# The SSM's input by channel in runs of 32 numbers, a gathered stationary operand, and state matrices in 2 KB rows

## Chip, cores and metric

The kernel runs on one core of one Trainium2 chip. The metric is device time in microseconds. The kernel before took 1888.09 us (median of three runs, 1886.04 to 1891.85).

## What is computed

`x` has 8 sequences of 2048 positions and 256 channels, in float32. Three sublayers follow each other:

```python
x = x + 0.5 * ffn(layernorm(x), w1, b1, w2, b2)      # 256 -> 1024 -> 256, relu
x = x + attn(layernorm(x))
x = x + 0.5 * ffn(layernorm(x), w1, b1, w2, b2)      # the same weights

def attn(u):        # a state space model (S4D): a long convolution by channel
    K[h, l] = 2 Re(sum_n Ct[h, n] exp(dt[h] A[h, n] l))      # 64 complex states n per channel
    y = causal convolution of u with K along the positions
    r = u + y + u * D
    return layernorm(r) * ln_w + ln_b
```

## The kernel before

**Two feed-forwards and the SSM between them.** The 2048 positions are cut into 16 chunks of 128; a chunk of one sequence is a column, so there are 128 columns, and 64 groups of two columns. `sublayer` (L807) runs a feed-forward over the groups. A group has 8 steps, each one block of 128 of the hidden layer: six matmuls (L788) into a PSUM bank, relu and a rounded copy `hh` on ACT (L857, L858), the remainder `hl` on DVE (L859); three steps later six matmuls (L798) take `hh` and `hl` to the output. `hh` and `hl` have four slots each. In the first feed-forward (letter a) `post_a` then adds the residual (L905), normalises each column (L696 on DVE, L692 on ACT in the first 12 groups) and writes it to `u`. In the second (letter b) `pre_b` reads columns of `u` from the last to the first: their statistics (L663) and a scaling (the instructions shown at L118).

**`u`** (L127) holds the SSM's input, later its output in place, as [position in chunk, chunk, sequence, channel], 128 KB per partition. A channel's 128 numbers on a partition lie 1024 bytes apart. Until the columns are written, quarters of `u` serve as room for making the SSM's matrices: `room[2]` and `room[3]` are the third and fourth quarters of the chunks.

**The matrices** are made during the first feed-forward by the generator `matrices` (L234). For each of 32 batches of 8 channels, POOL multiplies tables (`make`, L570 to L580), the result is stored (`o_dram`) and transposed by DMA through 16-bit planes (`spread`, `turn`, L590 to L605), put together again by a copy on DVE and one on ACT (`transpose`, L620, kept in program order) and stored as `pt_dram`. The generator yields how much of the feed-forward its work is to be spread over; `sublayer` adds 1.32 to a clock per step and takes work from the generator up to it. At certain groups (`due`) all the work up to a mark is issued at once if it has not come yet: the mark "half" (the matrices of the first half, which lie in `room[2]`) at group 39, "tables" at group 48. The clock decides the order of the program. The framework's scheduler may then reorder instructions that are not kept in order.

**The SSM** works on pairs of channels, in 12 groups of 8 or 16 pairs (`PLAN`, L920), whose states lie in three buffers A, B and E.
- `states(gr)` (L964): for each batch of 4 pairs and each channel c of the pair, `pt` is loaded (256 KB) and four float32 matmuls (L970) stream `u`'s channel through it: 15 chunks of 8 sequences, 120 columns. ACT keeps the result (L957).
- `scan` (L987): 14 steps over the chunks, of four small instructions (L1005 to L1008), some pairs on DVE and some on POOL. On DVE its two temporaries come from slots `hh` and `hl`, or, every other group, from `e` and `te`.
- `outputs(gr)` (L1019): for each batch and c, four matmuls (L1036) with `u`'s channel as the stationary operand and the near lags `tz` as the moving one, and four (L1041) with the states and `ot`; ACT writes the bank back to `u` (L1045). `ot` and `tz` are loaded before, 256 KB each.

The program has the states of groups 1, 2 and 3 first, and then outputs of a group and states of the group three later in turns. The states of group 0 come early, at the end of the first feed-forward (`early`, L1050, matmuls L1072). Each float32 matmul shows as two in the profile (64 batches x 4 x 2 = 512 for L1036). Loads and stores are issued by SP in one queue.

Of the kernel before, what the change touches and what calls it, by code (L numbers as in the profile page):

```python
# [10 lines left out]
F32 = mybir.dt.float32  # L11
F32R = mybir.dt.float32r
# [17 lines left out]
# pi / 2 in four parts, the first three of eight bits each  # L30
# [13 lines left out]
def macaron_s4d_kernel(  # L44
# [63 lines left out]
    BUFS = {"e": 1, "te": 1, "x": 5, "xn": 1, "xh": 2, "xl": 2, "hh": 4, "hl": 4, "pl": 2, "g": 1, "gt": 1}  # L108
# [11 lines left out]
    def ts(o, a, s0, op0, s1, op1):  # L120
# [5 lines left out]
    # The SSM's input, then its output in place: [position in chunk, chunk, batch, channel].  # L126
    u = upool.tile([P, NJ, B, H], F32, name="u")  # L127
    # Until their quarters of the input come: room for the SSM's matrices.
    room = [
        u[:, i * JQ : (i + 1) * JQ].rearrange("p j b h -> p (j b h)") for i in range(NQ)  # L130
    ]

    # ------------------------------------------------------------- weights
# [61 lines left out]
    # w**128, and its imaginary part with the signs for the conjugate states  # L195
# [27 lines left out]
    def vsqrt(o, v, t, s, pace):  # L223
        """o = sqrt(v), to float32's precision."""
# [9 lines left out]
    def matrices():  # L234
        S1 = 0.9              # two steps of 128 columns
        S2 = 1.35             # two steps of 256 columns
# [7 lines left out]
        # ---- parameters: (c, n) to the partitions  # L244
# [23 lines left out]
        # w and w**16: exp(dt A) and exp(16 dt A)  # L268
# [18 lines left out]
        # (no effect but where float32 holds no fraction of the phase)  # L287
# [19 lines left out]
        # the quadrant: q mod 4 as f in -2..2, cos = 1 - |f|, sin = f (2 - |f|)  # L307
# [12 lines left out]
        # w = rho (cs + i sn)(cq + i sq)  # L320
# [25 lines left out]
        # w**128  # L346
# [5 lines left out]
        # Ct = C (w - 1) / A, doubled  # L352
# [30 lines left out]
        # p0 = sqrt(2 Ct w)  # L383
# [28 lines left out]
        yield from vsqrt(fa, v, tt, s, S1)      # the larger part over sqrt(big)  # L412
# [19 lines left out]
        # ---- lag 0, with the skip and the residual: K[0] + 1 + D  # L432
# [23 lines left out]
        # ---- w**(16 a) and p0 w**b  # L456
# [27 lines left out]
        # ---- lags 128 to 1: Re(sum_n p0 w**(16 a) p0 w**b), eight pairs to a product, of  # L484
        # which the blocks on the diagonal count
# [71 lines left out]
        def make(bt):  # L557
            """P of a batch of channels."""
# [24 lines left out]
        def spread(bt):  # L583
            """Stores it, and turns its planes."""
# [28 lines left out]
        def transpose(bt):  # L613
# [3 lines left out]
            pu = ptb.bitcast(U16).rearrange("p (s r n w) -> p w r s n", s=BCH, r=2, w=2)  # L617
            plv = pl.rearrange("p w (r s n) -> p w r s n", r=2, n=N)
# [37 lines left out]
    # ------------------------------------------------------------ the sublayers  # L656
# [13 lines left out]
    def root(mv, name):  # L670
        """half of sqrt(var + eps)"""
# [4 lines left out]
    def rstds(mv, s, name):  # L676
        """1 / sqrt(var + eps), the root improved by a step."""
# [23 lines left out]

    def ucols(g):
        c0 = g * NTB
        return [u[:, (c0 + i) // B, (c0 + i) % B, :] for i in range(NTB)]
# [4 lines left out]
    def ffn_in(xt, name, on_act=False, by_dma=False):  # L709
        """Normalises xt and transposes it, in two parts; xt gets half the second bias."""  # L710
# [31 lines left out]
    def turn_by_dma(xn, name):  # L742
        """The transposes by the DMA engines: of the numbers' upper and lower halves."""
# [63 lines left out]
    def sublayer(w1t, w2t, pre, post, lead, tag, first=(), background=(), due=()):  # L807
        """A feed-forward over all groups. pre(g) makes a group's input in steps, the last
        of them `lead` steps after the first, just before the group's turn; post(g) takes
        its output in steps. `first` is work for the steps before the first group;  # L810
        `background` fills gaps: all of it up to a mark comes before the output of the
        group that `due` has for the mark."""
# [4 lines left out]
        last = {}             # the background is not to come before these  # L817
# [27 lines left out]
        for t in range(-lead, NG * SLOTS + LAG + 1):  # L845
# [3 lines left out]
            if t >= 0 and g < NG:  # L849
                fc = 2 * k + f  # L850
                hh = slot("hh", [P, TOK], f"hh_{tag}{g}_{fc}", F32R)
                hl = slot("hl", [P, TOK], f"hl_{tag}{g}_{fc}", F32R)
                pend[g, fc] = hh, hl
                ph = bank("h", f"ph_{tag}{g}_{fc}")[:, 0:TOK]
                up(w1t, xT[g], ph, fc)
                # the hidden block stays in PSUM until it is split
# [33 lines left out]
    # ---- x1 = x + ffn(norm(x)) / 2; u = norm(x1)  # L890
    ACT_NORM = 12         # groups during which the vector engine has the parameters to make
# [36 lines left out]
    TAGS = ("hh", "hl"), ("e", "te")  # L928
# [9 lines left out]
    # how many steps each group's scan keeps behind the one before it  # L938
# [15 lines left out]
    def keep(xs, pv, c, p0, cols):  # L954
        """The chunks' own states from PSUM: the pair's channels one below the other."""
# [6 lines left out]
    def states(gr):  # L962
        xs = states_of(gr)
        for p0, bt, c in batches(gr):  # L964
            pt = slot("x", [P, PB, P], f"pt{bt}_{c}")
            nc.sync.dma_start(out=pt, in_=pt_dram[bt].rearrange("k (l c m) -> k l c m", c=2, m=P)[:, :, c])
            pv = bank("tbo"[(2 * bt + c) % 3], f"pv{bt}_{c}")
            pv = pv[:, 0 : PB * CB].rearrange("p (l m) -> p l m", l=PB)
            for l in range(PB):
                nc.tensor.matmul(  # L970
                    pv[:, l, :], pt[:, l, :], u[:, 0 : NJ - 1, :, BCH * bt + 2 * l + c],
                    start=True, stop=True,
                )
            keep(xs, pv, c, p0, slice(B, NJ * B))
# [12 lines left out]
    def scan(gr, E, p0, p1, j0, j1, tags):  # L987
        """state of a chunk += conj(w**128) times the state of the chunk before it"""
# [6 lines left out]
        for j in range(j0, j1):  # L995
            t1, t2 = (
                slot(tag, [P, 2, 8 if tag in ("g", "gt") else 16, B], f"{tag}_{gr}_{j}")[:, :, 0:n] for tag in tags
            )
# [14 lines left out]
    def stack(xs, pairs, sw):  # L1013
        """Puts each channel's real and imaginary parts one below the other."""
# [4 lines left out]
    def outputs(gr):  # L1019
        xs = states_of(gr)  # L1020
        for p0, bt, c in batches(gr):
# [6 lines left out]
            # tz[k, l, 127 - i] = K[i - k]  # L1028
# [4 lines left out]
            )  # L1033
            py = bank("h", f"py{bt}_{c}").rearrange("p (l m) -> p l m", l=PB)
            for l in range(PB):
                nc.tensor.matmul(  # L1036
                    py[:, l, :], u[:, :, :, BCH * bt + 2 * l + c].rearrange("p j b -> p (j b)"), tz[:, l, :],
                    start=(l == 0), stop=False, skip_group_check=True,
                )
            for l in range(PB):  # L1040
# [5 lines left out]
                u[:, :, :, BCH * bt + c : BCH * (bt + 1) : 2],  # L1046
                py.rearrange("p l (j b) -> p j b l", b=B),
            )

    def early():  # L1050
# [138 lines left out]
```

## Time and profile before

| | before |
|---|---|
| runs, median (lowest to highest) | 1888.09 us (1886.04 to 1891.85) |
| profiled execution, span | 1885.0 us, granted clock 0.987 |
| PE busy (matmuls) | 1813.4 us, 96% |
| DVE, ACT, POOL busy | 1566.6, 1267.4, 726.0 us |
| DMA moved | 245 MB, 130 GB/s over the span |
| first feed-forward | to about 866 us (last L905) |
| SSM's stage, first L970 to last L1041 | 843 to 1125 us |
| second feed-forward | from about 1131 us |

Of the profiled execution the span is given, from its first to its last instruction; the runs' median lies 3.1 us above it. A row of the profile's groups names the line of the kernel, the engine, the operation, output and inputs by the program's names and their shape. PE is TensorE's matmuls, PEld its weight loads, which overlap the matmuls. SP is the queue that issues the DMAs.

### The profile page before, as it was taken

How to read it: one execution, taken by the hardware profiler on the slowest of the kernel's cores; microseconds unless marked ns; L12 is line 12 of the kernel's file. 1: busy time of each engine (PE TensorE's matmuls, PEld its weight loads, DVE VectorE, ACT ScalarE, POOL GpSimd, SP SyncE). 2: the span in 40 equal slices, each digit the busy share in tenths (PEclk: the TensorE clock that was granted, in tenths of full speed). 3: DMA queues.
4: the chain of work that ended last, by engine and by line, in shares of the span. 5: the costliest groups of instructions: out<-in, count | busy, mean ns of one | idle time of the engine just before them, and what ended most of it. 6: DMA issues, size and time to landing. Idle time of an engine off the chain costs nothing.

```text
span 1885.0 us, 41022 instructions
## 1 busy us (share of the span) xinstructions
PE 1813.4 (96%) x14091; PEld 1797.2 (95%) x14091; DVE 1566.6 (83%) x5027; ACT 1267.4 (67%) x3027; POOL 726.0 (39%) x963
## 2 busy tenths in 40 slices
PE   7999899889989999999999988999999999999999
PEld 7998889889988999999999988999999999999998
DVE  5999897988899867757666648999888999999995
ACT  6776556767767767766566645767777776677775
POOL 1117753888488115111866621222222222222220
PEclk9999999999999999999999998999999999999999
DMA  5111224798879743345667681333333333333331
GB/s 188 45 45 50 80 80 129 215 251 243 242 224 254 207 107 94 92 118 162 174 179 198 183 246 51 91 90 94 94 94 90 92 95 90 92 94 91 93 93 52
DMA packets 329140, 245.31 MB, mean 130 GB/s; under 512 B 170467, under 2 KB 275683, under 8 KB 328419
## 3 DMA queue, kind: packets, MB, share of 16 engines
q1 hardware_dynamic: 327152, 241.76, 45.9%
q8 instruction: 111, 1.82, 0.4%
q0 software_dynamic: 800, 0.67, 0.2%
q14 instruction: 99, 0.80, 0.1%
q10 hardware_dynamic: 978, 0.26, 0.1%
HBM read 91.89 MB, written 111.15 MB: 108 GB/s over the span
## 4 chain that ended last, share of the span: by engine, by line
PE 65%; DVE 2%; DMA 1%; issue 0%; ACT 0%; DVEq 0%; ACTq 0%
PE po_b L798 19%; PE ph_b L788 19%; PE po_a L798 7%; PE ph_a L788 6%; PE py L1036 6%; PE pv L970 5%; PE py L1041 3%; DMA tz<-kpad 1%; PE pe L1072 0%; DVE hl_a L859 0%; DVE xb L118 0%; DVE st_r L663 0%; DVE u L620 0%; DVE y L118 0%; DVE u L696 0%
## 5 line engine op out<-in xcount | busy, mean ns | idle before, releaser
L788 PE MATMUL ph_a<-xh_a,wa 128*128 128x256 f32 x2048 | 460.2, 289 | 7.6 <-ACT xh_a L735 3.7
L788 PE MATMUL ph_b<-xh_b,wb 128*128 128x256 f32 x2048 | 442.4, 284 | 0.7 <-ACT xh_b L735 0.7
L798 PE MATMUL po_a<-wa,hh_a 128*128 128x256 f32 x2048 | 393.3, 285 | 0.0
L798 PE MATMUL po_b<-wb,hh_b 128*128 128x256 f32 x2048 | 387.5, 283 | 0.0
L788 PEld LDWEIGHTS ph_a<-xh_a,wa 128*128 128x128 f32 x2048 | 361.7, 196 | 9.2 <-ACT xh_a L735 5.6
L857 ACT ACTIVATE ph_a<-ph_a,b_sb 128x256 f32<-128x256 f32 x512 | 228.8, 449 | 189.5 <-PE ph_a L788 179.1
L788 PEld LDWEIGHTS ph_b<-xh_b,wb 128*128 128x128 f32 x2048 | 352.5, 193 | 1.1 <-ACT xh_b L735 1.1
L857 ACT ACTIVATE ph_b<-ph_b,b_sb 128x256 f32<-128x256 f32 x512 | 230.3, 451 | 162.2 <-PE ph_b L788 151.4
L798 PEld LDWEIGHTS po_a<-wa,hh_a 128*128 128x128 f32 x2048 | 323.2, 194 | 0.2 <-issue 0.2
L798 PEld LDWEIGHTS po_b<-wb,hh_b 128*128 128x128 f32 x2048 | 319.2, 192 | 0.0
L788 PE MATMUL ph_a<-xl_a,wa 128*128 128x256 f32 x1024 | 294.4, 290 | 20.7 <-DVE xl_a L769 11.2
L798 PE MATMUL po_a<-wa,hl_a 128*128 128x256 f32 x1024 | 299.6, 293 | 9.0 <-DVE hl_a L859 8.5
L1125 POOL TENSOR_TENSOR xb<-xb,lnb_sb 128x512 f32<-128x512 f32 x64 | 94.4, 1475 | 530.6 <-DMA xb<-x_dram 329.0
L798 PE MATMUL po_b<-wb,hl_b 128*128 128x256 f32 x1024 | 292.7, 286 | 0.3 <-DVE hl_b L859 0.2
L788 PE MATMUL ph_b<-xl_b,wb 128*128 128x256 f32 x1024 | 286.5, 284 | 0.1
L859 DVE TENSOR_TENSOR hl_a<-ph_a,hh_a 128x256 fp32r<-128x256 f32 x512 | 206.9, 411 | 82.6 <-ACT hh_a L858 80.9
L859 DVE TENSOR_TENSOR hl_b<-ph_b,hh_b 128x256 fp32r<-128x256 f32 x512 | 205.1, 410 | 37.6 <-ACT hh_b L858 36.0
L788 PEld LDWEIGHTS ph_a<-xl_a,wa 128*128 128x128 f32 x1024 | 201.3, 197 | 23.1 <-DVE xl_a L769 12.2
L719 POOL TENSOR_TENSOR xa<-xa,hb 128x512 f32<-128x512 f32 x64 | 84.3, 1317 | 350.6 <-DVE xn_a L696 239.3
L798 PEld LDWEIGHTS po_a<-wa,hl_a 128*128 128x128 f32 x1024 | 198.5, 194 | 14.4 <-DVE hl_a L859 14.0
L798 PEld LDWEIGHTS po_b<-wb,hl_b 128*128 128x128 f32 x1024 | 196.3, 192 | 1.6 <-DVE hl_b L859 0.8
L788 PEld LDWEIGHTS ph_b<-xl_b,wb 128*128 128x128 f32 x1024 | 197.2, 193 | 0.4 <-DVE xl_b L737 0.3
(281 smaller groups left out, 3589.7 us busy)
## 6 DMA issues: line engine op xcount, KB each, us to landing
xa<-in_L_attn_x_dram SPq DMA_DIRECT2D x64, 256.0 KB, 2.8
x_dram<-xa SPq DMA_DIRECT2D x64, 256.0 KB, 2.3
o<-u SPq DMA_DIRECT2D x64, 256.0 KB, 4.0
pv<-planes SPq DMA_DIRECT2D x32, 512.0 KB, 3.5
pt<-u SPq DMA_DIRECT2D x32, 512.0 KB, 3.6
ot<-o SPq DMA_DIRECT2D x64, 256.0 KB, 3.5
tz<-kpad SPq DMA_DIRECT2D x64, 256.0 KB, 3.8
xb<-x_dram SPq DMA_DIRECT2D x64, 256.0 KB, 2.8
```

The costliest lines, as they stand in the source:

```text
L719: G_.tensor_add(xt, xt, hb2.unsqueeze(1).to_broadcast([P, NTB, H]))
L788: nc.tensor.matmul(ph, wt[wp][:, dc, fs], xp[:, dc, :], start=(n == 0), stop=(n == 3 * NDC - 1))
L798: nc.tensor.matmul(po[:, i, :], hp[:, tsl], wt[wp][:, fc, :], start=(fc == 0 and i == 0 and n == 0), stop=(fc == NFC - 1 and n == 2), skip ...
L857: A_.activation(ph, ph, AF.Relu, bias=b1_sb[:, fc : fc + 1])
L859: last[V] = V.tensor_sub(hl, ph, hh.bitcast(F32))
L970: nc.tensor.matmul(pv[:, l, :], pt[:, l, :], u[:, 0 : NJ - 1, :, BCH * bt + 2 * l + c], start=True, stop=True,)
L1036: nc.tensor.matmul(py[:, l, :], u[:, :, :, BCH * bt + 2 * l + c].rearrange("p j b -> p (j b)"), tz[:, l, :], start=(l == 0), stop=False, s ...
L1041: nc.tensor.matmul(py[:, l, :], xs[:, c, p0 + l, :], ot[:, l, :], start=False, stop=(l == PB - 1), skip_group_check=True,)
L1125: G_.tensor_add(xt, xt, lnb_sb.unsqueeze(1).to_broadcast([P, NTB, H]))
```

## The change

- `u` becomes [position in chunk, quarter, channel, 32 columns]: a channel's 128 numbers on a partition lie in four runs of 32. A column's 256 channels now lie 128 bytes apart, and a column spreads over the whole of its quarter.
- L970's matmuls stream all four runs, 128 columns in place of 120; the last 8 are not kept.
- In `outputs` a DVE copy gathers the four channels of a batch into a contiguous tile `uc` ([128, 4, 128]), which is then the stationary operand of L1036.
- `hh` and `hl` become the two halves of one tile `hx` with four slots. The scan's temporaries on every other group, and `uc`, come from `hx` too.
- `pt_dram` is put in the order (c, pair, column) instead of (pair, c, column): a load of `pt` takes 2 KB in a row from each partition's row instead of four times 512 bytes. The copies of L620 write in that order.
- The mark "half" is due at group 32 instead of 39.

Everything else is as it was. The core of the diff, without removed comments:

```diff
-    BUFS = {"e": 1, "te": 1, "x": 5, "xn": 1, "xh": 2, "xl": 2, "hh": 4, "hl": 4, "pl": 2, "g": 1, "gt": 1}
+    BUFS = {"e": 1, "te": 1, "x": 5, "xn": 1, "xh": 2, "xl": 2, "hx": 4, "pl": 2, "g": 1, "gt": 1}
...
-    u = upool.tile([P, NJ, B, H], F32, name="u")
+    CQ = JQ * B
+    u = upool.tile([P, NQ, H, CQ], F32, name="u")
...
+    room = [u[:, i].rearrange("p h m -> p (h m)") for i in range(NQ)]
...
-            pu = ptb.bitcast(U16).rearrange("p (s r n w) -> p w r s n", s=BCH, r=2, w=2)
-            plv = pl.rearrange("p w (r s n) -> p w r s n", r=2, n=N)
+            pu = ptb.bitcast(U16).rearrange("p (c l r n w) -> p w r l c n", c=2, r=2, n=N, w=2)
+            plv = pl.rearrange("p w (r l c n) -> p w r l c n", r=2, c=2, n=N)
...
+    def column(c):
+        return u[:, c // CQ, :, c % CQ]
...
-                hh = slot("hh", [P, TOK], f"hh_{tag}{g}_{fc}", F32R)
-                hl = slot("hl", [P, TOK], f"hl_{tag}{g}_{fc}", F32R)
-                pend[g, fc] = hh, hl
+                hx = slot("hx", [P, 2, TOK], f"hx_{tag}{g}_{fc}", F32R)
+                hh, hl = pend[g, fc] = hx[:, 0], hx[:, 1]
...
-    TAGS = ("hh", "hl"), ("e", "te")
+    TAGS = ("hx",), ("e", "te")
...
-            nc.sync.dma_start(out=pt, in_=pt_dram[bt].rearrange("k (l c m) -> k l c m", c=2, m=P)[:, :, c])
+            nc.sync.dma_start(out=pt, in_=pt_dram[bt].rearrange("k (c l m) -> k c l m", c=2, m=P)[:, c])
...
-                    pv[:, l, :], pt[:, l, :], u[:, 0 : NJ - 1, :, BCH * bt + 2 * l + c],
+                    pv[:, l, :], pt[:, l, :], u[:, :, BCH * bt + 2 * l + c, :],
...
-            keep(xs, pv, c, p0, slice(B, NJ * B))
+            keep(xs, pv[:, :, 0:CB], c, p0, slice(B, NJ * B))
...
+            if tags == ("hx",):
+                both = slot("hx", [P, 2, 2, 16, B], f"hx_{gr}_{j}")
+                t1, t2 = (both[:, i, :, 0:n] for i in range(2))
...
+            mine = u[:, :, BCH * bt + c : BCH * (bt + 1) : 2, :]
+            uc = slot("hx", [P, PB, P], f"uc{bt}_{c}")
+            V.tensor_copy(
+                uc.rearrange("p l (q m) -> p l q m", q=NQ), mine.rearrange("p q l m -> p l q m")
+            )
...
-                    py[:, l, :], u[:, :, :, BCH * bt + 2 * l + c].rearrange("p j b -> p (j b)"), tz[:, l, :],
+                    py[:, l, :], uc[:, l, :], tz[:, l, :],
...
             A_.copy(
-                u[:, :, :, BCH * bt + c : BCH * (bt + 1) : 2],
-                py.rearrange("p l (j b) -> p j b l", b=B),
+                mine.rearrange("p q l m -> p l q m"),
+                py.rearrange("p l (q m) -> p l q m", q=NQ),
             )
...
-        {"half": 39, "tables": NG * 3 // 4},
+        {"half": NG // 2, "tables": NG * 3 // 4},
```

More of the change, by code (lines that the diff above doesn't have):

```diff
@@ L124, in macaron_s4d_kernel @@
     make_identity(nc, ident)
-    u = upool.tile([P, NJ, B, H], F32, name="u")
-    room = [
-        u[:, i * JQ : (i + 1) * JQ].rearrange("p j b h -> p (j b h)") for i in range(NQ)
-    ]
+    CQ = JQ * B
+    u = upool.tile([P, NQ, H, CQ], F32, name="u")
+    room = [u[:, i].rearrange("p h m -> p (h m)") for i in range(NQ)]
     wa1 = wpool.tile([P, 2, NDC, W], F32R, name="wa1", tag="wA")
@@ L700, in hbm @@
         return ap[b0 : b0 + NTB, j * P : (j + 1) * P, :].rearrange("b p h -> p b h")
+    def column(c):
+        return u[:, c // CQ, :, c % CQ]
     def ucols(g):
-        c0 = g * NTB
-        return [u[:, (c0 + i) // B, (c0 + i) % B, :] for i in range(NTB)]
+        return [column(g * NTB + i) for i in range(NTB)]
     def halves(xt):
@@ L965, in states @@
             pt = slot("x", [P, PB, P], f"pt{bt}_{c}")
-            nc.sync.dma_start(out=pt, in_=pt_dram[bt].rearrange("k (l c m) -> k l c m", c=2, m=P)[:, :, c])
+            nc.sync.dma_start(out=pt, in_=pt_dram[bt].rearrange("k (c l m) -> k c l m", c=2, m=P)[:, c])
             pv = bank("tbo"[(2 * bt + c) % 3], f"pv{bt}_{c}")
-            pv = pv[:, 0 : PB * CB].rearrange("p (l m) -> p l m", l=PB)
+            pv = pv.rearrange("p (l m) -> p l m", l=PB)
             for l in range(PB):
                 nc.tensor.matmul(
-                    pv[:, l, :], pt[:, l, :], u[:, 0 : NJ - 1, :, BCH * bt + 2 * l + c],
+                    pv[:, l, :], pt[:, l, :], u[:, :, BCH * bt + 2 * l + c, :],
                     start=True, stop=True,
                 )
-            keep(xs, pv, c, p0, slice(B, NJ * B))
+            keep(xs, pv[:, :, 0:CB], c, p0, slice(B, NJ * B))
         on_dve = sizes[gr] - POOL_PAIRS[gr]
@@ L995, in scan @@
         for j in range(j0, j1):
-            t1, t2 = (
-                slot(tag, [P, 2, 8 if tag in ("g", "gt") else 16, B], f"{tag}_{gr}_{j}")[:, :, 0:n] for tag in tags
-            )
+            if tags == ("hx",):
+                both = slot("hx", [P, 2, 2, 16, B], f"hx_{gr}_{j}")
+                t1, t2 = (both[:, i, :, 0:n] for i in range(2))
+            else:
+                t1, t2 = (
+                    slot(tag, [P, 2, 8 if tag in ("g", "gt") else 16, B], f"{tag}_{gr}_{j}")[:, :, 0:n]
+                    for tag in tags
+                )
             with ExitStack() as behind:
@@ L1033, in outputs @@
             )
+            mine = u[:, :, BCH * bt + c : BCH * (bt + 1) : 2, :]
+            uc = slot("hx", [P, PB, P], f"uc{bt}_{c}")
+            V.tensor_copy(
+                uc.rearrange("p l (q m) -> p l q m", q=NQ), mine.rearrange("p q l m -> p l q m")
+            )
             py = bank("h", f"py{bt}_{c}").rearrange("p (l m) -> p l m", l=PB)
@@ L1045, in outputs, with some @@
             A_.copy(
-                u[:, :, :, BCH * bt + c : BCH * (bt + 1) : 2],
-                py.rearrange("p l (j b) -> p j b l", b=B),
-            )
+                mine.rearrange("p q l m -> p l q m"),
+                py.rearrange("p l (q m) -> p l q m", q=NQ),
+            )
+    def some(j0, j1):
+        if (j1 - j0) % JQ == 0:
+            return u[:, j0 // JQ : j1 // JQ]
+        q = j0 // JQ
+        return u[:, q : q + 1, :, (j0 - q * JQ) * B : (j1 - q * JQ) * B]
     def early():
@@ L1067, in early @@
                         nc.sync.dma_start(
-                            out=pt, in_=pt_dram[bt].rearrange("k (l c m) -> k l c m", c=2, m=P)[:, l0 : l0 + 2, c]
+                            out=pt, in_=pt_dram[bt].rearrange("k (c l m) -> k c l m", c=2, m=P)[:, c, l0 : l0 + 2]
                         )
@@ L1073, in early @@
                                 pv[:, i, l, :], pt[:, l - l0, :],
-                                u[:, j0:j1, :, BCH * bt + 2 * l + c],
+                                some(j0, j1)[:, :, BCH * bt + 2 * l + c, :],
                                 start=True, stop=True,
@@ L1125, in pre_b @@
         G_.tensor_add(xt, xt, lnb_sb.unsqueeze(1).to_broadcast([P, NTB, H]))
-        uc = [u[:, i // B, i % B, :] for i in range(P - 1 - i0, P - 1 - i0 - NTB, -1)]
+        uc = [column(i) for i in range(P - 1 - i0, P - 1 - i0 - NTB, -1)]
         mv = stats(uc, f"r{g}", PIN & 2)
```

## The prediction

> **What bounds the kernel now.** I read the page first, then busy time by stretches, then the rows of the three matmuls that read the SSM's input `u`, then the chain of waits through their stage.
>
> Busy time by stretches (columns: the stretch and its length, busy us of each engine with its instructions, granted clock, DMA share, GB/s):
>
> ```profile
> core 0: us, PE busy (x) PEld busy (x) DVE busy (x) ACT busy (x) POOL busy (x), PEclk, DMA share, GB/s
> 320.00:640.00 320.00, 292.58 (x2294) 285.64 (x2293) 290.27 (x767) 228.99 (x503) 229.75 (x186) 0.96 0.88 239
> 680.00:840.00 160.00, 159.87 (x1326) 159.66 (x1325) 115.57 (x417) 113.08 (x290) 35.98 (x58) 1.00 0.34 97
> 880.00:1110.00 230.00, 228.33 (x1300) 227.40 (x1300) 154.89 (x561) 135.18 (x234) 152.07 (x453) 1.00 0.69 196
> 1160.00:1860.00 700.00, 700.00 (x5816) 699.12 (x5815) 641.89 (x2048) 494.06 (x1273) 168.81 (x120) 1.00 0.34 91
> ```
>
> TensorE is full in three of the four. Between 320 and 640, where the first feed-forward shares the engines with the making of the matrices, it stands still for 27 us, and DVE (91%) and DMA (88%) are as loaded. In the SSM's stage (880 to 1110) PE works 99% at full clock, with everything else at 59 to 69%: PE alone sets that stage's length. The rows of its three matmuls (min/median/max ns, first and last start in us):
>
> ```profile
> L1036 PEld LDWEIGHTS py<-tz,u x512: 291/312/363, 878.8 to 1124.0; 128*128 128x128 f32 x171
> ...
> L970 PE MATMUL pv<-u,pt x480: 362/382/452, 843.3 to 1091.6; 128*128 128x120 f32 x160
> ...
> L1041 PEld LDWEIGHTS py<-ot,xsA x192: 189/192/208, 910.7 to 1087.4; 128*128 128x128 f32 x192
> ```
>
> L1036 loads a channel of `u` as the stationary operand, one number every 1024 bytes; L1041 loads a contiguous operand of the same shape: 312 against 192 ns. L970 streams the same strided channel. These durations overlap, so the pace is read from unbroken pieces of the chain of waits (start us, us, what):
>
> ```profile
> 866.00 13.16 PE pv L970 x64
> ...
> 887.51 1.75 PE py L1036 x8
> ...
> 911.07 1.80 PE py L1041 x16
> ...
> 912.89 3.79 DMA tz<-kpad
> ```
>
> 13.16 / 64 = 0.206 us for L970, 1.75 / 8 = 0.219 for L1036, 1.80 / 16 = 0.1125 for L1041. The strided ones run at half the contiguous pace. The last row is an example of the only other thing on this chain, waits for `tz` (12% of the chain from 860 to 960).
>
> **The change, part by part.** Sums are made against the profiled execution's span of 1885.0 us; the runs' median, 1888.09, lies 3.1 us above, and I carry that over.
>
> *Strided operands gone.* PE's demand in the stage: 512 x 0.219 + 480 x 0.206 + 512 x 0.1125 = 112 + 99 + 58 = 269 us. Afterwards the moving channel is four runs of 32 numbers and the gathered stationary is contiguous, so I give all three L1041's pace, the nearest row; 128 columns instead of 120 in L970 are within it: 1504 x 0.1125 = 169 us. PE is relieved of 100 us. If runs of 32 streamed only at the strided pace, L970 would take 0.206 x 128/120 = 0.22 and the relief would be 48; I take 100, because 120 columns cost 0.206 with one number per read and a run offers 32. The early states (L1072), 32 matmuls of 96 columns and 32 of 24 while PE is full, gain 0.08 us each on the wide ones: 2.6 us.
>
> *What is late next.* By then PE asks 169 us, ACT (170 us busy from 843 to 1137: 68 keeping states, 57 stacking, 41 writing outputs) about the same, POOL's scans 139 without one 12 us wait. DVE's scans were busy 167 us, from 863.2 to 1111.1, most of their idle time spent on ACT's kept states, hence on PE's L970. DVE is therefore the next bound, and the change adds to it.
>
> *The gather.* 64 copies of 128x512 float32 from `u`. Below: the contiguous DVE rows L347 (copy of 128 numbers, 222 ns) and L306 (256 numbers, 276 ns) give 0.42 ns per further number, so 0.38 us. Above: the 128x512 tensor_tensor L737, 0.68. I take 0.55, between them since POOL's scans run at the same time and lengthen DVE rows (L1005 on 192 numbers: 0.35 alone, 0.45 to 0.49 beside POOL): 64 x 0.55 = 35 us (24 to 44), on DVE's FIFO among the scans. Each needs an `hx` slot, of which there are four, shared with the scans of every other group; a gather that waits for its slot holds the scan steps queued behind it on DVE, and PE's L1041 waits for those.
>
> So DVE needs 167 + 35 + about 7 of the feed-forward's tail = 209 us from 863.2. With no idle time the last scan step would end at 1072; PE kept 99% only because the others had a third to spare, and here four engines stand at 65 to 95%, so I take 95%: 220 us, 1083. From the last scan step to the last output matmul it was 14 us (1111.1 to 1125.1); four or five batches at 1.8 us of PE and 512 KB of DMA each leave about 10. The stage ends near 1093 instead of 1125: **-32 us** (DVE at 100%, -43; at 90%, -20).
>
> *2 KB rows for the state matrices.* The Trainium skill, DMA: Bandwidth & Descriptors, section Specifications, gives 512 B as the smallest transfer at line rate, by which rows four times as long bring nothing. The DMA packets of this trace in the stage have a median of 27 ns for 512 B and 84 ns for 2 KB: 108 against 84 ns for the same 2 KB. 60 loads x (512 x 27 - 128 x 84) ns / 16 engines = 11.5 us less DMA time. I take the trace's figure, but at a share of 0.69 it lies beside other work: 0 us, and it keeps DMA below saturation when the stage shrinks. If PE waited on every load, it would be worth 0.2 us x 60 = 12.
>
> *Columns of `u` at a stride of 128 bytes.* DVE's normalisation (L696) now writes them and the second feed-forward's statistics and scaling (L663, L118) read them. The rule against this is in the Trainium skill, SBUF — State Buffer, section on Door 1, in its note on 16-byte lines: an access that goes to a new line each time pays a penalty, without a price for DVE. The trace has one such write, with the contiguous copy beside it:
>
> ```profile
> L481 DVE COPY u<-u x1: 273/273/273, 169.5 to 169.5; 128x128 f32<-128x128 f32 x1
> ...
> L347 DVE COPY wr_c<-u x1: 222/222/222, 111.0 to 111.0; 128x128 f32<-128x128 f32 x1
> ...
> L696 DVE TENSOR_SCALAR u<-xa,mv_u,t_u x104: 390/408/2040, 185.8 to 872.6; 128x256 f32<-128x256 f32 x104
> ```
>
> By the rule as a surcharge, 51 ns per 128 numbers, 0.1 us per instruction: 104 writes give 10 us to DVE in the first feed-forward, and 256 reads 26 us in the second, inside DVE's 58 us of slack there. But L481 took about 1 ns per number over a fixed part, and L696 already takes 408 ns for 256, as slow as bn_stats (409): nothing is left to lose. I take 0 and keep up to 10. A gain isn't excluded where a slower form no longer waits for POOL; no row sizes it. ACT's strided writes (24 in the first groups) and its stores of `py`, whose target already is scattered, are at 0 beside PE; so is the changed order of L620's copies, whose inner run of 64 stays (at most 0.2 us x 32).
>
> *`hh` and `hl` in one slot.* Both are released by the same three matmuls of L798, so 0 in the feed-forwards.
>
> *The mark "half" at group 32 instead of 39.* A column now spreads over a whole quarter, so all first-half matrices must be out before group 32. Adding up the yields to that mark gives 369 units; group 32's first output is step 32 x 8 + 3 = 259, where the clock stands at 259 x 1.32 = 342. So 27 units, 3.4 batches, are issued at once. They include three pairs of L620 copies, kept in program order on DVE and ACT, with their DMA transposes (5.5 us to landing), stores and POOL products. In the trace group 32's first output comes at about 452; the three pairs of copies start near 455, 467 and 476, and could not come much faster, DMA being 95% busy from 440 to 480. Waiting behind the copies on ACT and DVE are L857 to L859 of the next units, hence PE; on SP, the transposes (kept in order) stand before the loads of `xa`. Store, transpose and copy for the last two batches, some 7 us each, could end at 466 at best: about 14 us of waiting from 452, less one or two units in flight, less 4 us won back while the background is ahead (20 steps at 1.44 instead of 1.6 us). I take **+7** (0 to 18).
>
> Sum: 1888.1 - 32 - 2.6 + 7 = 1860.5, so 1860.
>
> **The rivals.**
> - *DVE bound, as above*: 1860. For it: DVE has the largest demand once L970 and L1036 halve. Chance 0.50, 1846 to 1874.
> - *PE's relief mostly kept*: gathers at 0.38 fall into the scans' gaps, DVE never idles: 863 + 167 + 24 + 7 = 1061, + 8; the stage ends 56 us earlier, the burst costs 3: 1833. Against it: every scan still waits for ACT. Chance 0.20.
> - *Relief given back*: with four engines near the same load and three buffers for `tz` and `ot`, DVE reaches 88%: 863 + 237 + 12 = 1112, -13, burst 7: 1879. The waits for `tz` above speak for it. Chance 0.18, half of it within 0.3%.
> - *Slower: the four `hx` slots serialise scan and output.* If gathers for a group are placed behind the scan of the group three ahead that holds the same slots, its L1036 can't start until that scan ends, and PE idles for it: 56 DVE instructions at 0.27 to 0.42, 15 to 23 us, say 20. Six groups use `hx`. Up to one such idle leaves a gain; from two (40 us against the 28 above) the kernel is slower; three give 1920, two 1900: 1910. Against it: scans are three groups ahead, and half use other slots. Chance 0.12.
>
> 0.3% is about what a measurement of this kernel tells from no change: 1882 to 1894. Faster 0.50 + 0.20 + 0.09 = 0.79, same 0.09, slower 0.12. The range 1828 to 1890 leaves out the slower case and the end of the second.
>
> **What would show it.** L1036's and L970's pieces of the chain at 0.11 us per matmul, L1036's loads at 192 ns; if not, step one is wrong. DVE above 85% in the stage with the chain passing through L1005 to L1008 and the gather; if PE is still full, the second rival holds. Gather rows at 0.4 to 0.7 us. PE idle of 5 to 15 us near group 32, released by L620's DMA. L696 at 408 ns; the second feed-forward unchanged at 11.56 us a group. Idle PE before L1036 for whole scans would mean the last rival.

## Result and the profile after

The changed kernel took 1931.60 us, the median of four runs (1929.17 to 1936.78), the kernel before 1889.97 us (four runs, 1886.04 to 1892.46). The ratio is 1.0223, with a 95% interval of 1.0203 to 1.0244: **slower by 2.2%**, where 1.5% faster was forecast. The profiled execution of after was the slowest of its four runs, 1936.78 us with a span of 1935.0, so its 50 us over the span of before are some 8 more than the medians give.

Where the 50 us lie is read at one instruction: the first group's residual in the second feed-forward (L1146 before, L1166 after). It starts at 1153.0 us before and at 1181.5 after. So 28.5 us are lost before it, where a gain of 28 was forecast, and 21.5 us after it (732.0 to 753.5 us until the end), where nothing was forecast. Its rows, before and after (ns min/median/max, first and last start in us):

```profile
L1146 DVE TENSOR_TENSOR xb<-po_b,xb x64: 677/687/692, 1153.0 to 1880.5; 128x512 f32<-128x512 f32 x64
...
L1166 DVE TENSOR_TENSOR xb<-po_b,xb x64: 673/691/707, 1181.5 to 1930.4; 128x512 f32<-128x512 f32 x64
```

Busy time by stretches of after, with the columns of the table shown for before:

```profile
core 0: us, PE busy (x) PEld busy (x) DVE busy (x) ACT busy (x) POOL busy (x), PEclk, DMA share, GB/s
320.00:640.00 320.00, 286.91 (x2266) 279.67 (x2265) 287.37 (x753) 225.34 (x497) 231.09 (x186) 0.96 0.87 235
880.00:1110.00 230.00, 145.97 (x1182) 141.30 (x1181) 172.01 (x589) 130.07 (x230) 158.52 (x445) 0.83 0.56 169
1190.00:1890.00 700.00, 691.06 (x5647) 680.91 (x5646) 685.49 (x1999) 481.29 (x1237) 174.49 (x118) 1.00 0.34 89
```

In the SSM's stage PE fell from 99% to 63%, yet nothing took its place: DVE stands at 75%, POOL at 69%, ACT at 57%, DMA at 56%. Where no engine is full, the order of the work may be what is waited for; the timelines below show that it is. In the second feed-forward (last row) DVE has become full: 98%, where it was at 92%.

The rows of the instructions that the forecast costed, after:

```profile
L1049 PEld LDWEIGHTS py<-tz,uc x512: 185/192/338, 915.6 to 1150.9; 128*128 128x128 f32 x171
...
L972 PE MATMUL pv<-u,pt x480: 274/275/552, 864.9 to 1105.6; 128*128 128x128 f32 x160
...
L1044 DVE COPY uc<-u x64: 412/428/1400, 915.0 to 1143.1; 128x512 f32<-128x512 f32 x64
...
L663 DVE BATCH_NORM_STATS2 st_r<-u x128: 560/614/648, 1152.8 to 1889.7; 128x6 f32<-128x256 f32 x128
...
L696 DVE TENSOR_SCALAR u<-xa,mv_u,t_u x104: 500/548/2169, 188.5 to 864.3; 128x256 f32<-128x256 f32 x104
...
L118 DVE SCALAR_TENSOR_TENSOR y<-u,mv_r,lnw_sb x128: 633/1198/1696, 1154.0 to 1896.5; 128x256 f32<-128x256 f32 x128
```

L663 and L118 on `u` in before:

```profile
L663 DVE BATCH_NORM_STATS2 st_r<-u x128: 402/409/428, 1126.1 to 1839.6; 128x6 f32<-128x256 f32 x128
...
L118 DVE SCALAR_TENSOR_TENSOR y<-u,mv_r,lnw_sb x128: 469/480/1590, 1127.0 to 1846.5; 128x256 f32<-128x256 f32 x128
```

The first two rows of after say that the matmuls became what was forecast: loads of 192 ns instead of 312, and 275 instead of 382 ns for L972 (L970 before). The gather took 0.43 us, less than the 0.55 taken. The last three say that DVE pays for columns 128 bytes apart: L663 614 instead of 409 ns, L696 548 instead of 408, and L118's `y` never under 633 where it was never under 469. The median of `y` rose far more, from 480 to 1198, but that is not the stride. Its two instructions of a group show as a pair in the timelines from 1200 to 1800 us: a pair beside no POOL instruction took 0.65 us for each (0.44 in before), a pair beside one 1.35 (0.95 in before; medians), and 38 of 50 pairs lay beside one where it was 15 of 52 in before. And two start times stand out: L972 first starts at 864.9 us, when the last L696 ends, where it started at 843.3; L1049 first starts at 915.6, where L1036 started at 878.8.

What PE did in that gap, by its timeline in after (start us, us, what, and in brackets the idle time before it with its releaser):

```profile
887.80 1.95 PE L972 MATMUL pv<-u,pt 128*128 128x128 f32 x16
915.57 2.08 PE L1049 MATMUL py<-tz,uc 128*128 128x128 f32 x8 [25.82 <-DVE uc L1044]
...
970.44 2.08 PE L1049 MATMUL py<-tz,uc 128*128 128x128 f32 x8 [16.33 <-DVE uc L1044]
...
1025.26 2.08 PE L1049 MATMUL py<-tz,uc 128*128 128x128 f32 x8 [18.80 <-DVE uc L1044]
...
1088.74 2.08 PE L1049 MATMUL py<-tz,uc 128*128 128x128 f32 x8 [14.81 <-DVE uc L1044]
...
1125.24 2.04 PE L1049 MATMUL py<-tz,uc 128*128 128x128 f32 x8 [8.83 <-issue]
```

Five times PE stands still, for 9 to 26 us and 84.6 us in all, until a gather has run. (For the last time the profile names no releaser, but its gather starts at 1124.7 us, and it ends like the others.) The gather itself takes under half a microsecond. What DVE did before the first one, by DVE's timeline in after:

```profile
913.93 0.36 DVE L1015 TENSOR_TENSOR xsB<-xsB,hx 128x192 f32<-128x192 f32 x1
914.33 0.36 DVE L1012 TENSOR_TENSOR hx<-xsB,wr_c 128x192 f32<-128x192 f32 x1
914.61 0.45 DVE L1013 TENSOR_TENSOR hx<-xsB,wi_c 128x192 f32<-128x192 f32 x1
914.98 1.43 DVE L1044 COPY uc<-u 128x512 f32<-128x512 f32 x3
```

L1012 to L1015 are a scan step (L1005 to L1008 before). Three gathers come in one piece, behind the products of the last of the 14 steps that the scan on `xsB` takes in `hx`. They read only `u`, which was complete 50 us earlier. All five idle spells end like this: the 14 steps in `hx` start at 892.0 (`xsB`), 949.3 (`xsA`), 1001.4 (`xsE`), 1068.6 (`xsB`) and 1109.2 us (`xsE`), and the first gathers follow at 915.0, 969.8, 1024.6, 1088.2 and 1124.7.

### The profile page after: what moved, and what is told of

Its sections match the earlier page's. It is cut to its first block, busy times and chain, and to the rows that moved or that the text cites. A ratio compares the mean times of both kernels' runs of the same rounds, so it can differ in the third digit from the quotient of the medians.

```text
span 1935.0 us, 41118 instructions
## 1 busy us (share of the span) xinstructions
PE 1746.8 (90%) x14091; PEld 1716.3 (89%) x14091; DVE 1661.0 (86%) x5091; ACT 1266.2 (65%) x3027; POOL 745.7 (39%) x963
## 3 DMA queue, kind: packets, MB, share of 16 engines
q1 hardware_dynamic: 302064, 241.76, 44.8%
## 4 chain that ended last, share of the span: by engine, by line
PE 36%; DVE 24%; ACT 4%; issue 3%; DMA 2%; DVEq 0%; ACTq 0%; SPq 0%
PE po_b L801 10%; PE ph_b L791 10%; PE po_a L801 6%; PE ph_a L791 6%; DVE y L118 3%; DVE hx_b L861 3%; DVE st_r L663 2%; PE py L1049 2%; DVE xn_b L696 2%; DVE xb L118 2%; PE py L1054 1%; DMA tz<-kpad 1%; DVE pl_b L750 1%; DVE xb L1166 1%; ACT ph_b L859 1%
## 5 line engine op out<-in xcount | busy, mean ns | idle before, releaser
L801 PE MATMUL po_a<-wa,hx_a 128*128 128x256 f32 x3072 | 459.1, 288 | 13.5 <-DVE hx_a L861 13.1
L801 PE MATMUL po_b<-wb,hx_b 128*128 128x256 f32 x3072 | 448.2, 286 | 8.8 <-DVE hx_b L861 8.3
L801 PEld LDWEIGHTS po_a<-wa,hx_a 128*128 128x128 f32 x3072 | 407.9, 194 | 19.2 <-DVE hx_a L861 18.7
L801 PEld LDWEIGHTS po_b<-wb,hx_b 128*128 128x128 f32 x3072 | 399.7, 192 | 19.0 <-DVE hx_b L861 16.8
L861 DVE TENSOR_TENSOR hx_a<-ph_a,hx_a 128x256 fp32r<-128x256 f32 x512 | 207.1, 412 | 77.8 <-ACT hx_a L860 75.2
L861 DVE TENSOR_TENSOR hx_b<-ph_b,hx_b 128x256 fp32r<-128x256 f32 x512 | 204.5, 409 | 15.3 <-ACT hx_b L860 14.5
L860 ACT CAST hx_a<-ph_a 128x256 fp32r<-128x256 f32 x512 | 187.0, 374 | 12.4 <-PE po_a L801 1.6
L860 ACT CAST hx_b<-ph_b 128x256 fp32r<-128x256 f32 x512 | 187.4, 373 | 11.4
L1049 PE MATMUL py<-tz,uc 128*128 128x128 f32 x512 | 75.4, 295 | 90.3 <-DVE uc L1044 76.5
L1049 PEld LDWEIGHTS py<-tz,uc 128*128 128x128 f32 x512 | 68.1, 207 | 93.3 <-DVE uc L1044 77.4
```

The source lines that it names most:

```text
L801: nc.tensor.matmul(po[:, i, :], hp[:, tsl], wt[wp][:, fc, :], start=(fc == 0 and i == 0 and n == 0), stop=(fc == NFC - 1 and n == 2), skip ...
L860: last[A_] = A_.copy(hh, ph)
L861: last[V] = V.tensor_sub(hl, ph, hh.bitcast(F32))
L1049: nc.tensor.matmul(py[:, l, :], uc[:, l, :], tz[:, l, :], start=(l == 0), stop=False, skip_group_check=True,)
```

## Experiments

**The theories.** *Slots* (the forecast's fourth rival): tiles of `hx` are handed out in the order of the program, in which the scan of a later group (14 steps, each taking one of the four slots) stands before the gathers of an output; so the first gathers get the slots of that scan's last steps, and PE waits. *Load*: 64 gathers are too much for DVE, or stand too far back in its queue among the scans. *Columns*: the second feed-forward is slower because DVE reads columns 128 bytes apart. *Late start*: since a column spreads over its quarter and L972 streams all 128 columns, the early states wait for the last normalisation.

Times are given as ratios to the kernel before, which was run beside each of them. The last columns are from the profiled executions: the start of the first residual in the second feed-forward, and the time from there to the end.

| kernel | ratio [95%] | first residual at | from there to the end |
|---|---|---|---|
| before | 1 | 1153.0 us | 732.0 us |
| after | 1.0223 [1.0203, 1.0244] | 1181.5 | 753.5 |
| e1: `uc` from slots of `x` | 0.9991 [0.9976, 1.0006] | 1123.4 | 755.5 |
| e2: gather on ACT | 1.0221 [1.0205, 1.0236] | 1176.5 | 747.5 |
| e3: contiguous reads in `pre_b` | 1.0132 [1.0113, 1.0151] | 1179.2 | 734.1 |
| e4: before, "half" at 32 | 1.0020 [1.0010, 1.0031] | 1155.2 | 733.9 |
| e5: e1 and states of 120 columns | 0.9933 [0.9919, 0.9948] | 1117.2 | 757.3 |
| e6: before, 2 KB rows | 1.0004 [0.9991, 1.0018] | 1157.5 | 731.8 |
| f1: e1 and columns copied by ACT | 0.9969 [0.9957, 0.9982] | 1123.8 | 757.8 |
| f2: e5 and f1 | 0.9890 [0.9867, 0.9914] | 1119.4 | 752.0 |
| g1: e5 and pairs copied by ACT | 0.9881 [0.9866, 0.9896] | 1116.0 | 747.5 |
| g2: e5 and L750 on ACT | 0.9975 [0.9959, 0.9991] | 1113.9 | 766.8 |

The last column alone is a rough price: after, e1, e2 and e5 have the same second feed-forward, and it reads 747.5 to 757.3 us there.

**e1_uc_in_x: another slot for the gather.**

```diff
-            uc = slot("hx", [P, PB, P], f"uc{bt}_{c}")
+            uc = slot("x", [P, PB, P], f"uc{bt}_{c}")
```

> The changed kernel, but the gathered tile takes its slot among the five of the state matrices' loads (x), not among the four hx that the scans use. Slots theory (a gather waits for its turn among the hx slots, and so for a whole scan of a later group): the 77 us that PE stands before L1049 for the gather go, the SSM's stage shortens by 50 to 80 us, the kernel comes to 1855 to 1885. Load theory (DVE simply has too much to do in the stage: scans 167 us and gathers 28): no more than 15 us are won, 1915 to 1930. Second feed-forward unchanged, 11.7 us a group.

The five slots of `x` hold the loads of `pt` in this stage (for the last group of `ot` and `tz` too), and no scan takes one. The same instructions, on the same engines: the first gather now starts at 875.1 us instead of 915.0, and the stage by stretches and the gather's row read so in e1:

```profile
875.00:1090.00 215.00, 175.00 (x1398) 169.61 (x1398) 192.28 (x661) 141.09 (x252) 154.35 (x450) 0.93 0.76 227
...
L1044 DVE COPY uc<-u x64: 411/427/559, 875.1 to 1081.2; 128x512 f32<-128x512 f32 x64
```

DVE is busy for 89% (third number after the length, behind PE and PEld), PE for 81%. PE's wait for `uc` (us, times, longest) in after and in e1:

```profile
PE py L1049 <- DVE uc L1044: 76.5, 5, 25.8
...
PE py L1049 <- DVE uc L1044: 0.6, 1, 0.6
```

The first residual comes 58 us earlier in the profile, which shows the slowest run of after and the fastest of e1; the ratio falls by 2.3%, 44 us of 1888. The slots alone cost that, as much as the whole of the loss (42 us).

**e2_gather_act: the gather off DVE, in the same slots.**

```diff
-            V.tensor_copy(
+            A_.copy(
```

> The changed kernel, but the gather runs on ACT, still in an hx slot. Slots theory: PE still stands for about as long before L1049, since ACT's copy waits for the same slots: 1920 to 1945. Queue theory (the gather is late because it stands behind scan steps in DVE's own queue, whatever its slot): the waits go, 1860 to 1885. Load theory: DVE is relieved of 28 us, 1900 to 1910.

Who PE's loads and matmuls of L1049 waited for (us, times), in e2:

```profile
  ACT uc L1044: 145.5, 11
```

In after the same line is "DVE uc L1044: 153.9, 10" (loads and matmuls count the same idle time twice). The gather has left DVE, and PE waits as long for it on ACT; the time is unchanged. What ACT waits for before its gathers (us, times):

```profile
  DVE xsA L1015: 15.2, 4
  DVE xsB L1015: 14.8, 8
  DVE xsE L1015: 6.9, 6
```

L1015 is the last instruction of a scan step, the one that releases the step's slot. ACT's first three gathers start at 908.43, 909.98 and 911.52 us, each within 0.05 us of the end of such an L1015 on DVE (908.40, 909.94, 911.49): one slot, one gather. ACT runs no scan, so neither DVE's load nor its queue holds them. That rules out the load theory for this stage: it is the slot, whichever engine does the copy.

**e3_contig_reads: the reads of the second feed-forward made contiguous.** The statistics and the scaling read 256 neighbouring numbers of `u` that aren't the column's.

```diff
-        uc = [column(i) for i in range(P - 1 - i0, P - 1 - i0 - NTB, -1)]
+        uc = [u[:, i % NQ, H - 8 :, :].rearrange("p h m -> p (h m)") for i in range(P - 1 - i0, P - 1 - i0 - NTB, -1)]
```

> The changed kernel, but the second feed-forward's normalisation reads 256 contiguous numbers of u (the last 8 channels' runs) in place of a column at a stride of 128 bytes; it computes with other numbers. Stride theory: L663 on u falls from 614 to 410 ns, the scaling from about 1200 to 480 or 640, a group from 11.7 to 11.56 us, 18 to 24 us less in the second feed-forward: 1907 to 1914. Rival (the second feed-forward is slower through the later arrival of its weights or another order): 1928 to 1936.

L663's row and a stretch of the second feed-forward in e3:

```profile
L663 DVE BATCH_NORM_STATS2 st_r<-u x128: 397/405/427, 1152.6 to 1867.8; 128x6 f32<-128x256 f32 x128
...
1170.00:1820.00 650.00, 649.29 (x5385) 647.12 (x5384) 621.76 (x1914) 458.56 (x1178) 155.20 (x112) 1.00 0.36 91
```

With 405 ns for L663 PE is full again (649 of 650 us, where e1 has 641.53), and 734.1 us from the first residual to the end are before's 732.0 within 2 us, so `hh` and `hl` in one slot cost nothing that shows there. The ratio is 0.9% below after's, 17 us: the reads at a stride cost that. The expectation missed in one point: `y` of L118 falls to a least time of 471 ns but not in its median, which is 1320; 49 of 52 pairs lie beside a POOL instruction there, so those long times are not the stride's.

**e4_half32: the mark "half" at 32, in the kernel before.**

```diff
-        {"half": 39, "tables": NG * 3 // 4},
+        {"half": NG // 2, "tables": NG * 3 // 4},
```

> The kernel before with one part of the change alone: the mark half due at group 32 instead of 39. My prediction: 7 us slower (0 to 18). Rival from the trace of the changed kernel (the groups' times stand 3 us further back at group 37 than at group 31): 2 to 4 us slower, 1892.

1.0020, so 4 us. By stretches PE works 14.72 us between 445 and 465 in e4, where it works 17.02 in before: the stall is where it was expected, and short. From group 0's residual to group 37's it is 504.7 us in e4, 501.1 in before and 505.0 in after, so after's loss there would be this mark alone. But the kernels that share after's first feed-forward up to there (e1 to e3, e5 and those built on them) read 501.2 to 504.6: the mark's price is read from the ratio, and L696's 140 ns more per write cost nothing that can be told from these few us.

**e6_rows_only: the 2 KB rows, in the kernel before.**

```diff
-            pu = ptb.bitcast(U16).rearrange("p (s r n w) -> p w r s n", s=BCH, r=2, w=2)
+            pu = ptb.bitcast(U16).rearrange("p (c l r n w) -> p w r l c n", c=2, r=2, n=N, w=2)
...
-            nc.sync.dma_start(out=pt, in_=pt_dram[bt].rearrange("k (l c m) -> k l c m", c=2, m=P)[:, :, c])
+            nc.sync.dma_start(out=pt, in_=pt_dram[bt].rearrange("k (c l m) -> k c l m", c=2, m=P)[:, c])
```

> The kernel before with one part of the change alone: the state matrices in 2 KB rows. My prediction: no difference, since the loads lie beside PE's work (1885 to 1889), and some 10 us less DMA time in the SSM's stage. Rival (a load that PE waits for shortens): up to 12 us faster. Rival on the other side (the reordered copies of L620 get dearer on DVE, which is nearly full where they run): 3 to 6 us slower.

1.0004: nothing, as forecast. The queue's row of e6 (packets, MB, share of 16 engines' span):

```profile
q1 hardware_dynamic: 302064, 241.76, 45.6%
```

Before has 327152 packets at 45.9%. Over spans of 1889.3 and 1885.0 us that is 861.5 against 865.2 us; after, with the same 2 KB rows, has 44.8% of 1935.0, 866.9 us. So 25,000 packets fewer save no DMA time that shows (the share's last digit is worth 2 us), where 11.5 us had been worked out from packet medians.

**e5_states_120: the early states without the last columns.** e1, and for the first groups L972 becomes two matmuls, of 96 columns and of 24: the 120 columns that are needed, which leave out the last chunk.

```diff
...
+                ch = BCH * bt + 2 * l + c
+                for o, r in (
+                    ((pv[:, l, 0 : 3 * CQ], u[:, 0:3, ch, :]), (pv[:, l, 3 * CQ : CB], u[:, 3, ch, 0 : CB - 3 * CQ]))
+                    if gr < 4 else ((pv[:, l, :], u[:, :, ch, :]),)
+                ):
+                    nc.tensor.matmul(o, pt[:, l, :], r, start=True, stop=True)
```

> The kernel of e1 (gathered tile in x), and the states of groups 1 to 3 stream only the 15 chunks that are kept, as 96 and 24 columns in two matmuls, so that they need not wait for the last chunk's normalised columns. Late-start theory (streaming 128 columns puts the SSM's first matmuls behind the last group of the first feed-forward): the first L972 moves from about 859 to 845 us and the last output matmul comes 5 to 12 us earlier, 1873 to 1880. Rival (the stage is bound by the scans and the POOL chain, not by its start): within 3 us of e1, 1882 to 1888.

The matmuls of the states (L977 in e5), and the stretches around the start of the stage, in e5:

```profile
L977 PE MATMUL pv<-u,pt x608: 187/275/550, 845.7 to 1050.9; 128*128 128x128 f32 x88, 128*128 128x96 f32 x64
...
842.00:866.00 24.00, 24.00 (x208) 24.00 (x207) 10.23 (x31) 16.95 (x42) 4.82 (x12) 1.00 0.44 133
```

The first one starts at 845.7 us, 2.4 us later than before's L970, though there are 128 matmuls more; PE is full at the seam, where after works 20.08 of the 24 us. The ratio falls by 0.6%, 11 us: the late start's price. The states at the end of the first feed-forward had read 120 columns, the first 15 chunks; with 128 they wait for the last chunk, which groups 60 to 63 write last.

**f1_act_columns and f2_both: ACT makes the columns contiguous for DVE.** f1 is e1 with this, f2 is e5 with this.

```diff
+    ycols = wpool.tile([P, 4, NTB, H], F32, name="ycols", tag="wE")
...
-        uc = [column(i) for i in range(P - 1 - i0, P - 1 - i0 - NTB, -1)]
+        c1 = P - 1 - i0
+        A_.copy(
+            ycols[:, g % 4],
+            u[:, c1 // CQ, :, c1 % CQ - 1 : c1 % CQ + 1].rearrange("p h i -> p i h")[:, ::-1],
+        )
+        uc = halves(ycols[:, g % 4])
```

> The kernel of e1, and in the second feed-forward ACT copies a group's two columns of u into a contiguous tile that DVE then reads. Stride theory: L663 back at 410 ns, a group at 11.55 to 11.6 us as before, 18 to 22 us less than e1: 1863 to 1868. Rival (any extra work per group on ACT or its longer chain costs the same again): 1880 to 1890.

> The edits of e5 and f1 together. If both theories hold and the two don't meet: 1853 to 1862. If the late start is not a cost: as f1.

The copy's row and a stretch of the second feed-forward in f1:

```profile
L1149 ACT COPY ycols<-u x64: 1058/1137/1173, 1093.9 to 1796.7; 128x512 f32<-128x512 f32 x64
...
1170.00:1820.00 650.00, 639.91 (x5209) 629.71 (x5209) 598.62 (x1841) 486.13 (x1192) 152.89 (x110) 1.00 0.33 89
```

DVE goes down to 92% from e1's 98%, which is before's load, and still the second feed-forward doesn't get shorter in the profile (757.8 against 755.5 us). By the ratios f1 gains 0.2% on e1 and f2 0.4% on e5, 4 and 8 us, where 18 to 22 were expected of the copy; f2's 1865.6 us also lie above its expectation. ACT took over 1.14 us of copying per group and is 75% busy, and its queue also holds the relu and `hx` of every step. DVE's load isn't the only thing that sets this pace.

**g1_act_pairs: the same copy in neighbouring pairs.** e5, with the two columns of a group kept as neighbours in `ycols`; DVE then reads every second number.

```diff
...
+        A_.copy(ycols[:, g % 4], u[:, c1 // CQ, :, c1 % CQ - 1 : c1 % CQ + 1])
+        uc = [ycols[:, g % 4, :, 1 - i] for i in range(NTB)]
```

> The kernel of e5, and in the second feed-forward ACT copies both columns of a group as they lie, two neighbouring numbers of each channel at a time, into a contiguous tile of pairs; DVE reads every second number of it. If it is the jump to a new place for each number that costs, the copy takes about 0.6 us where that of f1 took 1.14, L663 stays near 410 ns, and a group comes to 11.6 to 11.75 us: 1856 to 1866. Rival (any copy in ACT's queue between the steps of the hidden blocks costs what DVE wins, as in f1): 11.9 us a group, 1870 to 1878.

The copy and the statistics in g1:

```profile
L1151 ACT COPY ycols<-u x64: 627/657/693, 1084.7 to 1779.5; 128x512 f32<-128x512 f32 x64
...
L663 DVE BATCH_NORM_STATS2 st_r<-ycols x128: 400/409/428, 1085.3 to 1818.0; 128x6 f32<-128x256 f32 x128
```

Two numbers at a place cost ACT 0.66 us instead of 1.14, and a stride of 8 bytes costs DVE's statistics nothing (409 ns). From the first residual to the end it is 747.5 us against 757.3 in e5, and by the ratios g1 is 10 us faster than e5. Its 0.9881 is, with f2's 0.9890, the best of all: 22 us faster than before.

**g2_deint_act: DVE relieved in another place.** e5, with both copies of L750 in the second feed-forward on ACT.

```diff
-        for w, copy in DEINT:
+        for w, copy in DEINT if name[0] == "a" else ((0, A_.copy), (1, A_.copy)):
```

> The kernel of e5, and in the second feed-forward the copy of the lower halves for the DMA transposes (L750, 0.71 us a group on DVE) runs on ACT beside that of the upper halves; the strided reads stay. If DVE's load (98% there) sets the second feed-forward's pace: a group at 11.55 to 11.7 us, 1855 to 1864. Rival (ACT's queue becomes what PE waits for): no gain, 1872 to 1880.

What DVE waited for before L118 (us, times), and a stretch of the second feed-forward, in g2:

```profile
  ACT pl_b L750: 72.5, 60
...
1170.00:1820.00 650.00, 631.59 (x5162) 621.62 (x5161) 573.02 (x1775) 454.83 (x1184) 144.91 (x108) 1.00 0.34 88
```

DVE has only 88% left to do, and this is the slowest second feed-forward of all (766.8 us); at 1883.0 us the kernel is slower than either theory expected. DVE now waits 1.2 us per group for ACT's copies, and PE's share falls to 97%, the lowest of these kernels. "DVE is full, so take anything off it" fell here.

## Why the forecast was wrong

**The step that failed is the gather.** The forecast wrote that each gather "needs an `hx` slot, of which there are four, shared with the scans of every other group", and then put only 35 us of DVE time into the sum. The order in which slots are handed out went to a rival with a chance of 0.12, against which it held that "scans are three groups ahead, and half use other slots". The first half of that is the reason *for* the stall: belonging to a later group, the scan stands before the gathers in the program. The arithmetic was at hand: 15 to 23 us an idle, and "from two (40 us against the 28 above) the kernel is slower". Measured: five, of 8.8 to 25.8 us, each with the sign that the forecast had named for this rival. By e1 it is worth 44 us, by e2 it isn't DVE's load. That the 84.6 us of idle time are worth only 44 is in keeping with DVE's 89% in e1. The rival's 1910 us, with two or three idles of 20 us, are short of 1932 chiefly by the two steps below that it didn't contain.

**"Nothing is left to lose" for strided columns was wrong.** It was inferred from L696 taking 408 ns for 256 contiguous numbers, as if a slow instruction hid the stride. The stride came on top: 205 ns per 256 numbers read, 140 per 256 written. The rule that was set aside (the Trainium skill, SBUF — State Buffer, section on Door 1: an access to a new 16-byte line each time pays a penalty) was right. Even the surcharge of 0.1 us that the forecast derived for it was half of what L663 shows. And 128 x 0.205 us for L663 alone, 26 us, wasn't taken up by DVE's 58 us of slack, since e3 prices the reads at 17 us; which of the gaps they missed, no run shows. The writes, with DVE at 90%, cost nothing that could be told (e4). Nor did the gain come that the forecast left open here: the strided `y` of L118 takes 1.35 us beside POOL where the contiguous one takes 0.95 in before and 1.25 in e3.

**128 columns "are within" the pace, but they include late data.** The price of L972 per matmul was right, and what it has to wait for was overlooked: 11 us (e5).

**Right:** PE's relief (L1036 and L970 to the contiguous pace), the 2 KB rows at 0 for the kernel's time (e6; the 11.5 us less DMA time weren't there), the mark "half" at +7, measured 4 (e4), the gather's own 0.55 us, measured 0.43. DVE as the next bound is right in part. With the slots out of the way (e1) the last output matmul starts at 1091.2 us, where the stage's end was worked out at 1093, but that agreement is luck. DVE stands at 89% there, not 95%; e1 also holds the late start; and its chain from 860 to 1092 us, its pieces added up, lies 73 us on POOL's part of the scans, 56 on DVE, 52 on PE and 39 on DMA. Without the late start (e5) the last one starts at 1086.9, and DVE has the largest part of the chain, some 120 of 241 us, 16 of them the gather.

The sum by ratios, in us of 1888: 44 (slots) + 17 (reads) + 11 (late start) + 4 (mark) + 1 (rows) = 77; measured are +42, so -35 is left for relief and gather together, and the forecast had -32 and -2.6. This takes the effects as adding, which was not tried for each pair, and by the ratios' intervals the single terms are good to some 2 to 5 us and the rest to some 7; so the agreement is closer than the figures allow.

**Open:** what makes DVE's instructions longer beside POOL's. And why g1's second feed-forward takes 747.5 us when e3's, with no copy on ACT, takes 734.1. It may be the copy's length or its place in ACT's queue, as f1 and g2 suggest, or the order that the scheduler made of it (e2, with nothing changed in the second feed-forward, reads 747.5 too); no run separates these.

## What to carry to other kernels

A tile that joins a rotating set of buffers inherits the waits of everything that takes a slot before it in the program; before counting what its instruction costs, list in program order who holds each slot and until when. A stage with no engine above 75%, as here, may be waiting on such an order: a change of one buffer's name (e1) tests it. When a layout moves a stride from one engine to another, price the stride on the engine that gets it, and ask of a wider operand which late data it now includes.

## What the runs showed of the hardware

- DVE pays per number at a stride of 128 bytes: reading 256 float32 took 614 ns against 409 (0.8 ns each), writing them 548 against 408 (0.55 ns each). ACT's L692, writing them, took 839 ns against 592. At 8 bytes the statistics took the same 409 ns.
- DVE's L118 on a column took 0.44 us by itself and 0.95 beside a POOL instruction in before, 0.65 and 1.35 at the stride in after (medians of pairs).
- ACT's copy of 512 numbers took 1.14 us when each lay 128 bytes from the next, and 0.66 us in neighbouring pairs.
- TensorE streamed runs of 32 numbers as fast as a contiguous operand (275 ns for L972, as for L1054).
- Each idle spell costs more than its length: the granted clock was 0.50 for the first 2.4 us after the first spell and 0.65 in the next 2 us. The first eight matmuls of L1049 took 2.08 us there; later ones follow each other's start by 0.89 us for eight. Taking every stretch as a mixture of half and full clock, that is 3.4 to 5.8 us at half clock after each of the five spells, and 1.7 to 2.9 us lost. The Trainium skill (TensorE: Matmul & The Clock Gate, Part 1) has the array at half clock until it has worked for some 3.4 us; the shortest of the five agrees, the others took longer.

The stretches behind the last point, in after:

```profile
915.57:918.00 2.43, 2.43 (x11) 2.43 (x12) 2.31 (x6) 0.71 (x2) 2.19 (x7) 0.50 0.00 0
918.00:920.00 2.00, 2.00 (x14) 2.00 (x13) 0.11 (x1) 1.91 (x4) 1.76 (x7) 0.65 0.42 111
920.00:922.00 2.00, 2.00 (x20) 2.00 (x20) 0.52 (x1) 1.94 (x5) 1.76 (x6) 1.00 0.62 166
```
